# The last group's gated MLP, done for three tiles and then for the fourth

## The chip, the cores and the metric

The kernel runs on one core of a Trainium2 chip. The metric is the device time of one execution in microseconds (us), as the median of several executions; lower is better. Engines are named as the profile names them: PE is TensorE (PEld its weight loads), DVE is VectorE, ACT is ScalarE, POOL is GpSimd, SP issues the DMAs. SBUF is the on-chip memory, PSUM the memory into which PE writes.

## The reference, cut to what matters

The input x has 2 sequences of 1024 tokens with 128 channels. A stack of six blocks is applied to it, each behind a layer norm and added to x: a mixture of experts, an attention, the mixture again, a two-layer local transformer, a linear attention, and the same local transformer once more. The change is in the last block, in the second of its two layers:

```python
x = x + 0.5 * _L1_ffn_ref(_layernorm(x), ...)     # the last block: two layers of

def _layer(x, wqkv, qs, ksc, wo, lg, lb, w1, b1, w2, b2):
    ...                                           # local attention, gives o
    x = x + o @ wo
    h = shift_token(x)                            # channels 64.. from the token before
    mu = h.mean(-1, keepdims=True)
    var = h.var(-1, keepdims=True)
    h = (h - mu) / jnp.sqrt(var + 1e-05) * lg + lb
    h = h @ w1 + b1                               # 128 -> 682
    a, g = jnp.split(h, 2, axis=-1)               # 341 products, 341 gates
    h = a * jax.nn.gelu(g, approximate=False)
    x = x + h @ w2 + b2                           # 341 -> 128
    return x
```

So the gated MLP of a token needs the attention's result for this token and the one before it. All data are float32.

## The kernel before, in words

The 2048 tokens lie in 16 tiles of 128 tokens (one token a partition), eight a sequence. Four tiles make a group (`G = 4`); the function `local` works through the groups in the order of layer `l`, sequence `b` and half `c`, so (1, 1, 1) is the last group of a block. `x` holds the sum over blocks, `y` the running value inside the local transformer; both stay in SBUF.

The order of the work is written out by hand. `at(key, fn, *args)` puts a call into a plan, the plan is sorted by key, and the calls are made in that order; each engine executes its instructions in the order in which they were issued, waiting on semaphores for the others. A group starts at a key `n0`; tile k of it has the keys `n0 + k + d` with d from the list `per_tile`, and the group's MLP has `n0 + 7 + d` with d from `per_group`.

Per tile, the attention ends with these steps: `upright` (PE transposes the weights of attention, into two PSUM banks), `stood` (ACT copies them to SBUF), `weigh` (PE, 16 small matmuls `av_f`), `out_kept` (ACT copies the result to oT, L1171), `out_projected` (PE, `pj_f`, L1177), `added` (DVE adds it to the tile's y, L1183).

Per group, the MLP has: `lower_half` (POOL copies channels 0 to 63 of y to `h`, L1191), `shifted` (PE moves channels 64 to 127 down by one token: L1202, L1204, L1205), `upper_half` (ACT copies that to `h`, L1209), five pieces of the norm (`norm_h`: statistics on DVE L153 and L155, negative mean on POOL L158, root as Ln and Exp on ACT L162 and L163, offset on POOL L166, scaling on ACT L141, one instruction a tile), `inner_turned` (PE transposes, L1224), `inner_kept` (ACT, scale and shift of the norm, to `hn`, L1229), `gates` (PE: three chunks of gates of 128, 128 and 85 rows, L1239, and the third chunk of products, L1240), `gelus` (ACT, L1247; then the table of functions is set back for Ln and Exp), `third` (DVE multiplies the third products with their gates, L1253), `others` (PE: the first two chunks of products, `aa_f`, L1264), `first_two` (DVE, L1253), `outer` (PE: 12 matmuls to 128 channels, `po_f`, L1277), `second_bias` (POOL adds b2 to y, L1218) and `outer_added` (DVE adds `po_f` to y, L1288). In the last layer `onto_x` adds half of y to x (DVE, L1322) and, where `store` is set, which holds for the last block alone, issues the group's write to DRAM (SP, L1324).

In the last group all steps of the MLP have keys behind the `added` of its fourth tile. The late steps of group (1, 1, 0), from `others` on, fall in the same stretch.

PSUM has three rings: `bank2` gives pairs of banks from two buffers, `bankT` single banks from two, `bankO(name, 0 or 1)` two single ones. A new tile waits for the readers of the one that it replaces. SBUF tiles of one tag are reused in the same way; `t1` (1024 columns, two buffers) holds a tile's queries and keys until they are transposed.

Of the kernel before, what the change touches and what calls it, by code (L numbers as in the profile page):

```python
# [8 lines left out]
F32 = mybir.dt.float32  # L9
# [5 lines left out]
P = 128  # L15
# [16 lines left out]
def macaron_kernel(ctx: ExitStack, tc: tile.TileContext, a: dict, out: bass.AP):  # L32
# [14 lines left out]
    def bank2(name):  # L47
        return psA.tile([P, 2, 512], F32, tag="A", name=name)
# [6 lines left out]
    def bankO(name, which=None):  # L55
        if which is None:
            turn[0] ^= 1
            which = turn[0]
        return psO.tile([P, 512], F32, tag=f"O{which}", name=name)
# [890 lines left out]
    def at(key, fn, *args):  # L950
        plan.append((key, len(plan), lambda: fn(*args)))
# [5 lines left out]
    def tiles_of(b, c):  # L957
        return b * TB + G * c
# [7 lines left out]
    def local(name, steps, normed, store):  # L966
# [304 lines left out]
        def outer(l, b, c):  # L1271
            _, hh = mids.pop((l, b, c))
            w2 = lw[l][3]
            po = ps_["o", l, b, c] = bank2(f"po_{name}{l}{b}{c}")[:, 0, :]
            for t in range(G):
                for j, (o, n) in enumerate(HCH):
                    nc.tensor.matmul(  # L1277
                        po[:, t * P : (t + 1) * P],
                        lhsT=hh[:n, j, t * P : (t + 1) * P],
                        rhs=w2[:n, j, :],  # L1280
                        start=(j == 0),
                        stop=(j == 2),
                    )

        def outer_added(l, b, c):
            i0 = tiles_of(b, c)
            yf = y[:, i0 : i0 + G, :].rearrange("p t d -> p (t d)")
            nc.vector.tensor_tensor(yf, ps_.pop(("o", l, b, c)), yf, ALU.add)  # L1288

        per_tile = [  # L1290
            (-0.310, project), (-0.310, squares), (-0.048, cosines), (-0.024, sines), (0.212, least_norm),
# [12 lines left out]
        for (l, b, c), n0 in steps.items():  # L1304
            if l == 0:
                for part, d in enumerate(normed[b, c]):
                    at(d, norm, b, c, part)
            at(n0 - (0.626 if l == 0 else 1.519), channels, l, b, c)
            at(n0 + 0.307, keys_of_group, l, b, c)
            for k in range(G):  # L1310
                for d, fn in per_tile:
                    at(n0 + k + d, fn, l, b, G * c + k)
            for d, fn, *more in per_group:
                at(n0 + 7 + d, fn, l, b, c, *more)
            if l == 1:
                at(n0 + 11.707, onto_x, b, c, store)

    def onto_x(b, c, store):
# [380 lines left out]
```

## Time and profile before

| | us |
|---|---|
| median of 3 runs | 1902.21 (1901.45 to 1903.34) |
| the profiled execution's own time | 1902.45 |
| its span | 1900.7 |
| busy PE, DVE, ACT, POOL | 1831.6, 1402.9, 1136.0, 1136.9 |
| `added` of the fourth tile of the last group ends | 1878.3 |
| last write issued | 1897.38 |

Times inside the span count from its start. The page gives busy time and its share of the span for each engine; the chain that ended last follows the work back from the last instruction, at each step to what released it. In a list in order of time a row has start, duration, engine, line, operation, result and sources, the number of instructions merged into it and, in brackets, how long the engine had been idle and what ended that. A matmul in float32 appears as two records, a transpose as one. The ends of matmuls are modelled.

### The profile page before, as it was taken

Reading aid. Unit: us, or ns where it says so; the run is one execution under the profiler, and the core shown is the slowest. Engines: PE = TensorE matmul, PEld = TensorE weight load, DVE = VectorE, ACT = ScalarE, POOL = GpSimd, SP = SyncE. Lnnn points to the kernel's source line nnn. Section 1 sums busy time; section 2 is a strip of 40 time slices with the busy share of each in tenths; the row PEclk is TensorE's granted clock in tenths of the full one; section 3 lists DMA queues with packets and bytes.
Section 4 is the critical chain, followed back from the end, with each engine's and each line's share of the span. In section 5 each row is a group of like instructions: output and inputs, shape, how many; then the busy total and the mean of one; then the engine's idle time right before and its main releaser. Section 6 shows DMA issues by size and latency. Waiting matters only on the chain.

```text
span 1900.7 us, 37595 instructions
## 1 busy us (share of the span) xinstructions
PE 1831.6 (96%) x14482; PEld 1188.3 (63%) x14482; DVE 1402.9 (74%) x2450; ACT 1136.0 (60%) x2087; POOL 1136.9 (60%) x1036
## 2 busy tenths in 40 slices
PE   8999999999999999999999989999999899999997
PEld 5564666556665666556556556677756566676775
DVE  5748667776778667776763568888887788888884
ACT  3325555565566555565654457777676467677775
POOL 4544434343534434344444479888886689788883
PEclk8998999999999999999999999999999999999999
DMA  5331101010101101012013211111100000011110
GB/s 133 107 89 23 24 12 35 9 26 12 34 12 23 23 13 34 8 27 72 1 43 112 76 34 32 24 27 24 27 18 16 7 18 18 21 26 24 26 35 26
DMA packets 52414, 64.14 MB, mean 34 GB/s; under 512 B 17890, under 2 KB 26892, under 8 KB 51980
## 3 DMA queue, kind: packets, MB, share of 16 engines
q1 hardware_dynamic: 52236, 61.74, 12.7%
q8 instruction: 115, 1.88, 0.4%
q14 instruction: 63, 0.52, 0.1%
HBM read 27.89 MB, written 1.31 MB: 15 GB/s over the span
## 4 chain that ended last, share of the span: by engine, by line
PE 69%; ACT 12%; DVE 10%; POOL 5%; issue 4%; DMA 0%; SPq 0%; DVEq 0%; ACTq 0%; POOLq 0%
PE s L650 11%; PE tp L700 10%; PE av L717 9%; PE qk_f L989 4%; ACT p L679 4%; PE gu_m L284 3%; PE gu_m L285 3%; PE tp_f L1147 2%; PE pq L598 2%; PE acc_m L268 2%; PE s_f L1100 2%; PE av_f L1161 2%; PE v_f L1067 2%; PE po_f L1277 2%; PE tq_f L1056 2%
## 5 line engine op out<-in xcount | busy, mean ns | idle before, releaser
L686 POOL TENSOR_SCALAR p<-p,den 128x1024 f32<-128x1024 f32 x256 | 292.1, 1153 | 399.0 <-DVE den L684 313.8
L679 ACT ACTIVATE p<-p,nm 128x1024 f32<-128x1024 f32 x256 | 294.7, 1151 | 357.5 <-DVE nm L666 341.2
L666 DVE CUSTOM_DVE_ANT_0 p<-s,bias 128x1024 f32<-128x1024 f32 x256 | 302.7, 1219 | 104.0 <-PE s L650 101.4
L700 PEld LDWEIGHTS tp<-ident,p 128*128 128x128 f32 x2048 | 226.6, 141 | 100.2 <-issue 38.8
L700 PE MATMUL tp<-ident,p 128*128 128x128 f32 x2048 | 276.9, 278 | 12.2 <-ACT pt L704 10.8
L650 PE MATMUL s<-qk,qk 64*128 64x512 f32 x1024 | 258.0, 617 | 3.7 <-DVE nm L666 3.7
L717 PE MATMUL av<-pt,v 128*64 128x256 f32 x2048 | 249.1, 385 | 0.0
L706 DVE COPY pt<-tp 128x512 f32<-128x512 f32 x256 | 176.2, 688 | 92.6 <-PE tp L700 92.2
L717 PEld LDWEIGHTS av<-pt,v 128*64 128x64 f32 x2048 | 135.9, 136 | 150.0 <-issue 83.7
L1035 POOL TENSOR_TENSOR t_f<-t_f,t_f 128x1024 f32<-128x1024 f32 x64 | 151.2, 2362 | 13.6 <-DVE t_f L1021 10.0
L308 POOL TENSOR_TENSOR h_m<-h_m,cb_m 128x512 f32<-128x512 f32 x64 | 88.3, 1382 | 117.3 <-DVE h_m L304 81.5
L704 ACT COPY pt<-tp 128x512 f32<-128x512 f32 x256 | 147.5, 576 | 4.3 <-PE tp L700 3.9
L650 PEld LDWEIGHTS s<-qk,qk 64*128 64x128 f32 x1024 | 89.0, 186 | 88.1 <-issue 84.6
L1139 POOL TENSOR_TENSOR s_f<-s_f,sm_f 128x1024 f32<-128x1024 f32 x64 | 121.4, 1897 | 35.5 <-DVE sm_f L1135 33.4
L1040 POOL TENSOR_TENSOR t_f<-t_f,rn_f 128x1024 f32<-128x1024 f32 x64 | 122.3, 1911 | 12.3 <-ACT ktok L1471 8.5
L989 PE MATMUL qk_f<-wqkv,hT 128*128 128x512 f32 x256 | 123.8, 606 | 3.2 <-DVE hT L983 1.9
L1125 POOL TENSOR_TENSOR s_f<-s_f,mx_f 128x1024 f32<-128x1024 f32 x64 | 123.3, 1926 | 0.4 <-DVE mx_f L1120 0.4
L300 ACT ACTIVATE h_m<-gu_m 128x512 f32<-128x512 f32 x72 | 42.8, 597 | 127.3 <-PE gu_m L285 125.1
L1002 ACT ACTIVATE t_f<-qk_f 128x1024 f32<-128x1024 f32 x64 | 65.5, 1024 | 88.7 <-PE qk_f L989 68.8
L304 DVE TENSOR_TENSOR h_m<-h_m,gu_m 128x512 f32<-128x512 f32 x72 | 49.1, 684 | 80.8 <-ACT h_m L300 80.7
L614 POOL TENSOR_TENSOR rot<-rot,rot 128x512 f32<-128x512 f32 x32 | 40.7, 1271 | 88.0 <-DVE rot L609 88.0
L1152 ACT COPY pt_f<-tp_f 128x512 f32<-128x512 f32 x128 | 68.6, 586 | 40.4 <-PE tp_f L1147 39.6
(376 smaller groups left out, 3773.2 us busy)
## 6 DMA issues: line engine op xcount, KB each, us to landing
cb_m<-cwd_m SPq DMA_DIRECT2D x128, 128.0 KB, 3.0
qk<-rot SPq DMA_DIRECT2D x256, 64.0 KB, 2.0
tab<-in_xpos_dram SPq DMA_DIRECT2D x2, 1024.0 KB, 4.8
wqkv<-in_L_ffn_wqkv_dram SPq DMA_DIRECT2D x2, 768.0 KB, 6.4
x<-in_L_attn_x_dram SPq DMA_DIRECT2D x4, 256.0 KB, 3.5
wraw<-in_qkv_wT_dram SPq DMA_DIRECT2D x2, 512.0 KB, 4.9
vb_f<-vo_f SPq DMA_DIRECT2D x8, 128.0 KB, 2.3
out_dram<-x SPq DMA_DIRECT2D x4, 256.0 KB, 2.4
```

Source lines behind the costliest of these rows:

```text
L650: nc.tensor.matmul(pss[r][:, c, :], lhsT=qT[rows[r], t * P : (t + 1) * P], rhs=kT[rows[r], c * 512 : (c + 1) * 512], start=True, stop=True,)
L666: nc.vector.tensor_tensor_reduce(out=s, in0=pss[r].rearrange("p a n -> p (a n)"), in1=bias[r][:, o : o + S], scale=-1.0, scalar=3.0e38, op ...
L679: nc.scalar.activation(s, s, AF.Exp, bias=nm[:, r : r + 1], scale=-1.0, accum_out=den[:, r : r + 1])
L686: nc.gpsimd.tensor_scalar(probs[i, r], probs[i, r], den[:, r : r + 1], 1.0, ALU.mult, ALU.mult)
L700: nc.tensor.transpose(tp[:, k * P : (k + 1) * P], s[:, kb * P : (kb + 1) * P], ident)
L704: nc.scalar.copy(dst, src)
L706: nc.vector.tensor_copy(dst, src)
L717: nc.tensor.matmul(po[r * 64 : r * 64 + 64, 0 : 2 * P], lhsT=v[:, kb, r * 64 : r * 64 + 64], rhs=pts[i // 2, r, g][:, kb - 4 * g, :], star ...
L989: nc.tensor.matmul(ps[:, s, :], lhsT=hTs[b][:, n * P : (n + 1) * P], rhs=lw[l][0][:, s * INNER : (s + 1) * INNER], start=True, stop=True,)
L1035: nc.gpsimd.tensor_tensor(t1, t1, t2, ALU.add)
L1040: nc.gpsimd.tensor_tensor(t3, t3, rn.unsqueeze(2).to_broadcast([P, 2 * HL, 64]), ALU.mult)
L1125: nc.gpsimd.tensor_tensor(s3, s3, mx.unsqueeze(2).to_broadcast([P, HL, P]), ALU.subtract)
```

## The change

The last group of the last block no longer takes its MLP's steps from `per_group`. A new function `tail` plans them in two parts: "a", the first three tiles, and "b", the fourth.

- The lower half, shift, upper half and norm of part a have keys from the third tile's `added` on; the shift stands behind the last tile's `upright` and ahead of its `weigh`, the copy of the upper half behind `stood`, and the root and scaling behind `out_kept`.
- Everything else of the group, and the late steps of group (1, 1, 0) (`second_bias`, `others`, `first_two`, `outer`, `outer_added`, `onto_x`), stand behind the fourth tile's `added` in the order of the list `order`. The outer product of group (1, 1, 0) comes behind the gates of part a, its bias behind the norm of part b.
- Part a has gates with the third products, and the first two products later (`others_of`); part b has gates and all products in one step, in one pair of banks.
- The gates' results lie in two tiles of tag `t1` instead of one of tag `hh`, of which one is still in use by group (1, 1, 0). The outer products take banks of `bankO`.
- `bias` adds b2 to y, then `sums` adds half of y to x before the MLP's result is there; `done` adds half of the outer product to x, part by part, and issues a write for each: three tiles, then one.
- The table of functions is not set back after the last GELUs.

```diff
--- before.py
+++ after.py
@@ -1271,7 +1271,8 @@
         def outer(l, b, c):
             _, hh = mids.pop((l, b, c))
             w2 = lw[l][3]
-            po = ps_["o", l, b, c] = bank2(f"po_{name}{l}{b}{c}")[:, 0, :]
+            nm = f"po_{name}{l}{b}{c}"
+            po = ps_["o", l, b, c] = bankO(nm, 0) if store and (l, b, c) == (1, 1, 0) else bank2(nm)[:, 0, :]
             for t in range(G):
                 for j, (o, n) in enumerate(HCH):
                     nc.tensor.matmul(
@@ -1286,6 +1287,140 @@
             i0 = tiles_of(b, c)
             yf = y[:, i0 : i0 + G, :].rearrange("p t d -> p (t d)")
             nc.vector.tensor_tensor(yf, ps_.pop(("o", l, b, c)), yf, ALU.add)
+
+        def tail(n0, earlier):
+
+
+            l, b, c = 1, 1, 1
+            i0 = tiles_of(b, c)
+            ys, xs = y[:, i0 : i0 + G, :], x[:, i0 : i0 + G, :]
+            parts = {"a": slice(0, 3), "b": slice(3, 4)}
+            cols = {"a": slice(0, 384), "b": slice(384, 512)}
+            got = {}
+
+            def lower(p):
+                t = parts[p]
+                if p == "a":
+                    got["h"] = work.tile([P, G, C], F32, tag="h", name=f"h_{name}_last")
+                nc.gpsimd.tensor_copy(got["h"][:, t, 0:64], ys[:, t, 0:64])
+
+            def shift(p):
+                n = parts[p].stop - parts[p].start
+                sp = got["s", p] = bankT(f"sh_{name}_last{p}").rearrange("p (k d) -> p k d", d=64)[:, 0:n, :]
+                nc.tensor.matmul(sp, lhsT=down_one, rhs=ys[:, parts[p], 64:C], start=True, stop=False)
+                if p == "a":
+                    nc.tensor.matmul(sp[:, 0, :], lhsT=last_first, rhs=late[l, b], start=False, stop=False)
+                    sp, before = sp[:, 1:3, :], ys[:, 0:2, 64:C]
+                else:
+                    before = ys[:, 2:3, 64:C]
+                nc.tensor.matmul(sp, lhsT=last_first, rhs=before, start=False, stop=True)
+
+            def upper(p):
+                h = got["h"][:, parts[p], :]
+                nc.scalar.copy(h[:, :, 64:C], got.pop(("s", p)))
+                got["n", p] = norm_pieces(h, parts[p].stop - parts[p].start, f"f{name}_last{p}", h)
+
+            def norm_of(p, k):
+                got["n", p][k]()
+
+            def bias():
+                nc.gpsimd.tensor_tensor(ys, ys, lw[l][5].unsqueeze(1).to_broadcast([P, G, C]), ALU.add)
+
+            def sums():
+
+                nc.vector.scalar_tensor_tensor(xs, ys, 0.5, xs, ALU.mult, ALU.add)
+
+            def turn(p):
+                tp = got["t", p] = bankT(f"tf_{name}_last{p}")
+                for k in range(parts[p].start, parts[p].stop):
+                    nc.tensor.transpose(tp[:, k * P : (k + 1) * P], got["h"][:, k, :], ident)
+
+            def keep(p):
+                if p == "a":
+                    got["hn"] = work.tile([P, G * P], F32, tag="hn", name=f"hn_{name}_last")
+
+                    room = [work.tile([P, 1024], F32, tag="t1", name=f"hh{k}_{name}_last", bufs=2) for k in range(2)]
+                    got["hh", "a"] = [room[0][:, 0:384], room[0][:, 512:896], room[1][:, 0:384]]
+                    got["hh", "b"] = [room[1][:, (k + 4) * P : (k + 5) * P] for k in range(3)]
+                gb = lw[l][6]
+                hn, tp = got["hn"][:, cols[p]], got.pop(("t", p))[:, cols[p]]
+                nc.scalar.activation(hn, tp, AF.Identity, bias=gb[:, 1:2], scale=gb[:, 0:1])
+
+            def product(ps, o, m, p):
+                nc.tensor.matmul(ps, lhsT=lw[l][2][:, o : o + m], rhs=got["hn"][:, cols[p]], start=True, stop=True)
+
+            def gates_of(p):
+                first = bank2(f"ag_{name}_last{p}")
+                if p == "a":
+                    second, n = bank2(f"ah_{name}_last{p}"), 384
+                    gs = [first[:, 0, 0:n], first[:, 1, 0:n], second[: HCH[2][1], 0, 0:n]]
+                    vs = [None, None, second[: HCH[2][1], 1, 0:n]]
+                else:
+                    gs = [first[:m, 0, k * P : (k + 1) * P] for k, (_, m) in enumerate(HCH)]
+                    vs = [first[:m, 1, k * P : (k + 1) * P] for k, (_, m) in enumerate(HCH)]
+                for (o, m), ps in zip(HCH, gs):
+                    product(ps, HID + o, m, p)
+                for (o, m), ps in zip(HCH, vs):
+                    if ps is not None:
+                        product(ps, o, m, p)
+                got["g", p] = gs, vs
+
+            def gelus_of(p):
+                for k, ps in enumerate(got["g", p][0]):
+                    m = HCH[k][1]
+                    nc.scalar.activation(got["hh", p][k][:m], ps, AF.Gelu, bias=lw[l][4][:m, 1, k : k + 1])
+                written.append("gelu")
+
+            def gated_of(p, ks):
+                for k in ks:
+                    m, ps = HCH[k][1], got["g", p][1][k]
+                    hh = got["hh", p][k][:m]
+                    nc.vector.scalar_tensor_tensor(hh, ps, lw[l][4][:m, 0, k : k + 1], hh, ALU.add, ALU.mult)
+
+            def others_of(p):
+                ps = bank2(f"aa_{name}_last{p}")
+                for k in range(2):
+                    got["g", p][1][k] = ps[:, k, 0:384]
+                    product(ps[:, k, 0:384], k * P, P, p)
+
+            def outer_of(p):
+                po = got["o", p] = bankO(f"po_{name}_last{p}", 1 if p == "a" else 0)
+                for t in range(parts[p].start, parts[p].stop):
+                    for k, (_, m) in enumerate(HCH):
+                        nc.tensor.matmul(
+                            po[:, t * P : (t + 1) * P],
+                            lhsT=got["hh", p][k][:m, (t - parts[p].start) * P : (t - parts[p].start + 1) * P],
+                            rhs=lw[l][3][:m, k, :],
+                            start=(k == 0),
+                            stop=(k == 2),
+                        )
+
+            def done(p):
+                xp = xs[:, parts[p], :].rearrange("p t d -> p (t d)")
+                nc.vector.scalar_tensor_tensor(xp, got.pop(("o", p))[:, cols[p]], 0.5, xp, ALU.mult, ALU.add)
+                nc.sync.dma_start(out=ov[:, i0 + parts[p].start : i0 + parts[p].stop, :], in_=xs[:, parts[p], :])
+
+            off = {fn.__name__: d for d, fn in per_tile}
+            third_in = n0 + 2 + off["added"]
+            last_in = n0 + 3 + off["added"]
+            up, st, ok = (n0 + 3 + off[k] for k in ("upright", "stood", "out_kept"))
+            at(third_in + 0.0001, lower, "a")
+            at(max(third_in, up) + 0.0002, shift, "a")
+            at(max(third_in, st) + 0.0003, upper, "a")
+            at(max(third_in, st) + 0.0004, norm_of, "a", 0)
+            at(max(third_in, st) + 0.0005, norm_of, "a", 1)
+            for k in range(2, 5):
+                at(max(third_in, st, ok) + 0.0001 * (4 + k), norm_of, "a", k)
+            bias_, others_, first_two_, outer_, outer_added_, onto_ = earlier
+            order = [
+                others_, (lower, "b"), (shift, "b"), (upper, "b"), (turn, "a"), (keep, "a"), first_two_,
+                *[(norm_of, "b", k) for k in range(5)], bias_, (gates_of, "a"), (gelus_of, "a"), (bias,),
+                (gated_of, "a", (2,)), outer_, (turn, "b"), (keep, "b"), outer_added_, onto_, (sums,),
+                (others_of, "a"), (gated_of, "a", (0, 1)), (gates_of, "b"), (gelus_of, "b"),
+                (gated_of, "b", range(3)), (outer_of, "a"), (done, "a"), (outer_of, "b"), (done, "b"),
+            ]
+            for k, (fn, *more) in enumerate(order):
+                at(last_in + 0.0001 * (1 + k), fn, *more)
 
         per_tile = [
             (-0.310, project), (-0.310, squares), (-0.048, cosines), (-0.024, sines), (0.212, least_norm),
@@ -1310,9 +1445,14 @@
             for k in range(G):
                 for d, fn in per_tile:
                     at(n0 + k + d, fn, l, b, G * c + k)
+            ends = (second_bias, others, first_two, outer, outer_added)
             for d, fn, *more in per_group:
-                at(n0 + 7 + d, fn, l, b, c, *more)
-            if l == 1:
+                if not (store and l == b == 1 and (c == 1 or fn in ends)):
+                    at(n0 + 7 + d, fn, l, b, c, *more)
+            if store and l == b == 1:
+                if c == 1:
+                    tail(n0, [(fn, 1, 1, 0) for fn in ends] + [(onto_x, 1, 0, store)])
+            elif l == 1:
                 at(n0 + 11.707, onto_x, b, c, store)
 
     def onto_x(b, c, store):
```

## The prediction

> **What bounds the kernel now.** I read the page first, then the chain that ended last, then the instructions of the last 30 us in order of time, because the change touches nothing earlier: in the order of the two built programs every engine's stream is the same until the last tile's attention.
>
> ```profile
> span 1900.7 us, 37595 instructions
> ...
> PE 1831.6 (96%) x14482; PEld 1188.3 (63%) x14482; DVE 1402.9 (74%) x2450; ACT 1136.0 (60%) x2087; POOL 1136.9 (60%) x1036
> ...
> PE 69%; ACT 12%; DVE 10%; POOL 5%; issue 4%; DMA 0%; SPq 0%; DVEq 0%; ACTq 0%; POOLq 0%
> ...
> qk<-rot SPq DMA_DIRECT2D x256, 64.0 KB, 2.0
> ...
> out_dram<-x SPq DMA_DIRECT2D x4, 256.0 KB, 2.4
> ```
>
> TensorE (PE) is busy for 96% of the span and carries 69% of the chain, so over the whole run only less TensorE work would help. The tail is another regime: one group's MLP is alone and each engine waits for the one before it. These are its rows (start, duration, engine, line, operation), the first two of the group before:
>
> ```profile
> 1869.14 1.28 ACT L1247 ACT_TABLE_LOAD   x1
> ...
> 1870.44 1.26 ACT L1247 ACTIVATE hh_f<-ag_f,bi 128x512 f32<-128x512 f32 x2
> ...
> 1873.82 1.07 ACT L1152 COPY pt_f<-tp_f 128x512 f32<-128x512 f32 x2
> ...
> 1876.18 0.58 ACT L1171 COPY oT_f<-av_f 128x512 f32<-128x512 f32 x1 [1.29 <-PE av_f L1161]
> ...
> 1876.82 1.16 PE L1177 MATMUL pj_f<-wo,oT_f 128*128 128x128 f32 x8 [0.73 <-ACT oT_f L1171]
> ...
> 1877.81 1.88 PE L1264 MATMUL aa_f<-hn_f,wi 128*128 128x512 f32 x4
> ...
> 1879.73 1.41 DVE L1253 SCALAR_TENSOR_TENSOR hh_f<-aa_f,bi,hh_f 128x512 f32<-128x512 f32 x2 [1.43 <-PE aa_f L1264]
> ...
> 1880.13 0.54 PE L1205 MATMUL sh_f<-y,last_first 128*128 128x192 f32 x2
> ...
> 1881.20 2.72 PE L1277 MATMUL po_f<-w,hh_f 128*128 128x128 f32 x22 [0.17 <-DVE hh_f L1253]
> ...
> 1883.29 1.65 ACT L141 ACTIVATE h_f<-h_f,nb_ff,rs_ff 128x128 f32<-128x128 f32 x4 [0.38 <-POOL nb_ff L166]
> ...
> 1885.36 0.78 ACT L1229 ACTIVATE hn_f<-tf_f,gb 128x512 f32<-128x512 f32 x1 [0.42 <-PE tf_f L1224]
> ...
> 1886.15 1.28 ACT L1247 ACT_TABLE_LOAD   x1
> ...
> 1886.19 1.99 PE L1239 MATMUL ag_f<-hn_f,wi 128*128 128x512 f32 x4 [0.87 <-ACT hn_f L1229]
> ...
> 1888.21 1.26 ACT L1247 ACTIVATE hh_f<-ag_f,bi 128x512 f32<-128x512 f32 x2 [0.78 <-PE ag_f L1239]
> ...
> 1891.65 1.41 DVE L1253 SCALAR_TENSOR_TENSOR hh_f<-aa_f,bi,hh_f 128x512 f32<-128x512 f32 x2 [0.26 <-PE aa_f L1264]
> ...
> 1892.54 3.29 PE L1277 MATMUL po_f<-w,hh_f 128*128 128x128 f32 x24 [0.93 <-DVE hh_f L1253]
> ...
> 1895.94 0.69 DVE L1288 TENSOR_TENSOR y<-po_f,y 128x512 f32<-128x512 f32 x1 [2.88 <-PE po_f L1277]
> ...
> 1896.66 0.69 DVE L1322 SCALAR_TENSOR_TENSOR x<-y,x 128x512 f32<-128x512 f32 x1
> ...
> 1897.38 0.38 SPq L1324 DMA_DIRECT2D out_dram<-x  x1
> ```
>
> The reader is to see a single chain: oT copied at 1876.18, output projection, y, shift, statistics, normalisation (1883.29), hn (1885.36 to 1886.14), gates, GELUs, gating, outer product, two DVE passes, and the write issued at 1897.38. The span closes 3.3 us behind it. From 1886.14 TensorE waits three times, while its work for the group before (1881.20, 2.7 us) was done earlier, in the shade of the normalisation.
>
> One more row prices a product of 384 columns, which exists in the linear attention:
>
> ```profile
> 1385.67 1.56 PE L1374 MATMUL lp<-aw,xnTl 128*128 128x384 f32 x4
> ```
>
> Four records, of which a follower starts every 0.32 (512 columns: 0.43 each, from 1886.72, 1887.15, 1887.58 of the weight loads).
>
> **The change, part by part.** The sum goes against the profiled execution: span 1900.7 us, its own time 1902.45, 0.24 above the median of 1902.21, so a difference in span is taken off the median.
>
> Step 1: Shift of three tiles ahead of the last `weigh`. It needs y of the third tile (DVE 1873.49) and the bank that the first copy of 1873.82 frees (1874.36). The six records take 1.14 us in the row of 512 columns in all (1879.53 to 1880.67), 0.2 of it the result's way out; 384 columns take 0.21 less, so TensorE is free at 1875.14. In the old order `weigh` got going at 1874.94, when the second copy ended. Price 0.20, on the path. Queued behind it are `weigh`, oT and y of the fourth tile: oT ends 1876.96, its projection starts 1877.02. On ScalarE the copy of the shift (1875.4, 0.32) stands ahead of oT (1876.39), and ends in time. It could be nothing (both wait for the same copies) or 0.7 (the whole block); I take 0.20.
>
> Step 2: Norm of three tiles beside the last attention. Copy until 1875.7, statistics 3 x 0.31 until 1876.7, roots behind oT 1876.98 to 1877.5, POOL 0.35, three normalisations 1.27: done 1879.2. Their transposes come on TensorE behind projection (0.99), aa of the earlier group (4 x 0.43) and the fourth tile's shift (0.3), at 1880.03. Slack 0.8, so the norm costs nothing; what covers it is TensorE's own queue, and every us past those 0.8 would be paid. Transposes 0.35 and 0.2 on the way, then hn for 384 columns. A ScalarE row of 1024 elements takes 1024 ns and one of 512 597, 0.83 ns an element, so 0.78 becomes 0.67: 1880.64 to 1881.31. Gates of the three start at 1881.36 instead of 1886.19: 4.8 us earlier, the gain of the change.
>
> Step 3: What TensorE then has to do. In the new order: gates of three tiles 8 x 0.32 + 0.1 = 2.66; the earlier group's outer product, moved here, 24 records of 0.115 (22 in 2.72 less the way out) = 2.76; the fourth tile's transpose 0.12; the other two products 4 x 0.32 = 1.28; the fourth tile's six products 12 x 0.115 = 1.38, by the output projection's pace (8 records in 0.99, same shape). Sum 8.20, without a gap: until 1889.56. The bounds for the short product are 0.11 (transposes) and 0.43 (a 512-column one); the projection is the same shape, so its row is taken.
>
> Step 4: ScalarE. Statistics of the fourth tile come on DVE behind the earlier group's gating (until 1881.34); roots until 1882.25, POOL until 1882.6, normalised 1883.15, then the table load, 1.28, which began at 1886.15 and now begins at 1883.15. GELUs of three 1884.42 to 1885.96 (0.57, then 0.47 each, as 0.68 and 0.58 for 512). Third product gated on DVE until 1886.5, hn of the fourth tile 1887.1 to 1887.6, before TensorE asks for it at 1888.2. Slack 0.5 on both.
>
> Step 5: DVE, the next thing late. The earlier group's outer product now ends at 1886.98 instead of 1883.9. Behind it stand its addition, its sum onto x, and the new sum of y into x ahead, 0.72 each from the rows at 1895.94 and 1896.66; then the two gatings, 0.59 each (0.705 for 512 columns at 1.04 ns an element): until 1890.32. The sum ahead takes the place of one pass at the end, but here it is not free: TensorE is ready at 1889.56 and waits 0.8. POOL's two bias passes (1.27 each) run from 1882.7 to 1885.3, over 1.6 before DVE wants them; its bias of the earlier group, once at 1872.14, goes past nothing that is late.
>
> Step 6: The end. The first of the outer product's k = 1 matmuls starts at 1890.37; eleven more of 0.23 and 0.3: done 1893.2. GELUs of the fourth tile 1889.76 to 1890.64 and gatings until 1891.6 lie beside it, 0.6 ahead. One DVE pass of 128 columns, 0.28, instead of two of 0.69. Write issued at 1893.53: 3.85 earlier. SP gets one DMA more, its 0.38 lying before the last pass ends; the earlier group's write moves from 1885.40 to about 1888.4 and SP then has nothing until 1893. The last write is 64 KB instead of 256: the rows give 2.0 (rotary pieces) and 2.4. I take 2.05, 0.35 less; the bounds are nothing less, and 0.5 more if it queues behind the 192 KB issued at 1893.15.
>
> Sum: the gates start 4.83 earlier, with the 0.20 of step 1 already in it; from the gates to the write, 11.19 (1886.19 to 1897.38) becomes 12.17, so 0.98 is given back; the write gives 0.35. That is 4.2 us less, 1898.0.
>
> [...] The trace: the load at 1869.14 starts within 0.02 of the copy before it, takes 1.28, and the GELU follows at 1870.44. [...]
>
> **The rivals.**
> The table load holds the GELUs longer. Before, the product was what the GELU waited for (0.78 of idle at 1888.21), so an extra behind the load could have hidden there; now the products are ready at 1882.9 and nothing covers it. For it: the new place on the path. Against: 1870.44. A second length of the load, 1.28, would use up the 0.45 of DVE's slack and add 0.83: 1898.8. [...]
>
> Slower: weight loads set the pace of short products. Each product of the MLP loads weights, 0.19 us, and the next load starts 0.43 after the last. If that period were the load's and not the 512 columns', the fourth tile's shift and all products of both parts, 28 records, would take 0.43 each: 12.0 instead of 5.5, so TensorE ends 6.5 later, 0.8 of it inside DVE's lateness, and the write of 1893.5 comes at 1899.2: 1903.7. It decides from (5.5 + 0.8 + 4.2) / 28 = 0.38 a record. Against: four loads of the 384-column row in 0.94, and the projection's eight in 0.97.
>
> The gain is hidden. If y's fourth tile and not hn were what ends last, the three tiles would win nothing and the split only add. For it: both parts share TensorE's queue behind the same oT, and the last three matmuls need the fourth tile. Against: step 4 and 6 put the fourth tile 0.5 and 0.6 ahead everywhere. Each us it is later beyond that is paid; the whole gain needs 4.8. A delay of 1.5 gives 1899.0.
>
> **How the numbers follow.** The forecast has 0.84, by itself 1896.8 to 1899.2: 0.4 for the paces of steps 1 to 3, 0.3 for the short DVE and ScalarE forms, 0.3 for the write, and the spread of 1901.45 to 1903.34 on both kernels. Table load 0.06, hidden gain 0.05, weight loads 0.05. To leave out no more than 2 in 10 the range goes to 1896.3 and 1900.8. A change under 0.2%, 3.8 us, is about what a measurement of this kernel can't tell from none; the forecast lies 0.4 beyond that, so 0.70 of its 0.84 count as faster and 0.14 as no change. The table load and a hidden gain (0.11) are no change; of the weight loads 0.01 is too, and 0.04 is left for slower, for a pace above 0.43.
>
> **What would show it.** In the new profile: shift of three tiles at 1874.4 and oT not over 0.3 later; gates of three at 1881.4; no gap in TensorE from there until 1889.6; GELU directly behind the table load near 1884.4; DVE's five passes back to back from 1887.0; the last write issued near 1893.5 and the span 4.2 shorter. It is wrong if gates start after 1882, if the products' followers start over 0.35 apart, or if the last three matmuls wait for the gating of the fourth tile.

## The result, and the profile after

The changed kernel takes 1897.67 us (median of 9 executions, 1896.18 to 1900.26) against 1902.85 (9 executions, 1901.45 to 1903.93) of the kernel before: a ratio of 0.9974, 95% interval 0.9965 to 0.9983. That is 5.2 us faster, where 4.2 was forecast; 1897.67 lies 0.3 under the 1898.0 of the forecast and in its range. The profiled execution took 1896.90, its span is 1895.2.

The page of the changed kernel, in the same lines as before: TensorE's sum went down by 3.7 us (1.1 of them in the last stretch told below, 19.27 to 18.19), the chain's shares are as they were, and of the four writes of 256 KB three are left (the fourth is now one of 192 KB and one of 64).

```profile
span 1895.2 us, 37645 instructions
...
PE 1827.9 (96%) x14498; PEld 1187.8 (63%) x14498; DVE 1402.1 (74%) x2454; ACT 1136.0 (60%) x2093; POOL 1137.6 (60%) x1039
...
PE 69%; ACT 12%; DVE 10%; POOL 5%; issue 4%; DMA 0%; SPq 0%; DVEq 0%; ACTq 0%; POOLq 0%
...
out_dram<-x SPq DMA_DIRECT2D x3, 256.0 KB, 2.4
```

The span is 5.5 us shorter, but not all of it belongs to the change. I measure the changed part from a mark that both kernels reach by the same instructions in the same order: the table load of line 127, behind which the last tile's attention ends. This load starts at 1872.52 in the trace before and at 1871.35 in the trace after. From it to the end of the span are 28.19 us before and 23.85 after: **4.34 us is what the change moved in these two profiles**. The other 1.17 us lie ahead of the mark, in code that is the same; the last section comes back to them. "The last stretch" is this time below, and "mark + 8.43" is a time counted from the mark. Two profiles of the changed kernel give 23.85 and 23.84 for it. The mark in the trace of the kernel before:

```profile
1872.52 1.28 ACT L127 ACT_TABLE_LOAD   x1
```

The last stretch of the changed kernel in order of time (start, duration, engine, line, operation, result and sources, count, and in brackets the idle time with what ended it):

```profile
1871.35 1.28 ACT L127 ACT_TABLE_LOAD   x1
...
1873.28 0.59 PE L1310 MATMUL sh_f_lasta<-y,down_one 128*128 128x192 f32 x2 [0.91 <-ACT pt_f L1152]
...
1873.88 0.44 PE L1316 MATMUL sh_f_lasta<-y,last_first 128*128 128x128 f32 x2
...
1874.24 0.34 PE L1161 MATMUL av_f<-pt_f,vb_f1116n 128*64 128x64 f32 x4
...
1875.50 0.58 ACT L1171 COPY oT_f<-av_f 128x512 f32<-128x512 f32 x1 [0.83 <-PE av_f L1161]
...
1876.89 1.26 ACT L141 ACTIVATE h_f_last<-h_f_last,nb_ff_lasta,rs_ff_lasta 128x128 f32<-128x128 f32 x3 [0.37 <-POOL nb_ff_lasta L166]
...
1879.24 0.50 PE L1336 MATMUL tf_f_lasta<-ident,h_f_last 128*128 128x128 f32 x3
...
1879.78 0.67 ACT L1347 ACTIVATE hn_f_last<-tf_f_lasta,gb 128x384 f32<-128x384 f32 x1
...
1880.50 1.56 PE L1350 MATMUL ag_f_lasta<-hn_f_last,wi 128*128 128x384 f32 x4 [0.76 <-ACT hn_f_last L1347]
...
1882.32 1.28 ACT L1371 ACT_TABLE_LOAD   x1
...
1883.19 2.84 PE L1278 MATMUL po_f<-w,hh_f 128*128 128x128 f32 x24
1883.62 1.05 ACT L1371 ACTIVATE hh_f_last<-ag_f_lasta,bi 128x384 f32<-128x384 f32 x2
...
1886.14 0.69 DVE L1289 TENSOR_TENSOR y<-po_f,y 128x512 f32<-128x512 f32 x1 [0.36 <-PE tf_f_lastb L1336]
...
1886.86 0.69 DVE L1462 SCALAR_TENSOR_TENSOR x<-y,x 128x512 f32<-128x512 f32 x1
...
1887.27 1.49 PE L1350 MATMUL ag_f_lastb<-hn_f_last,wi 128*128 128x128 f32 x12
1887.47 0.68 DVE L1331 SCALAR_TENSOR_TENSOR x<-y,x 128x512 f32<-128x512 f32 x1
...
1888.07 1.13 DVE L1378 SCALAR_TENSOR_TENSOR hh_f_last<-aa_f_lasta,bi,hh_f_last 128x384 f32<-128x384 f32 x2
...
1888.74 2.58 PE L1390 MATMUL po_f_lasta<-w,hh_f_last 128*128 128x128 f32 x18
...
1889.26 1.86 PEld L1390 LDWEIGHTS po_f_lasta<-w,hh_f_last 128*128 128x128 f32 x16 [0.23 <-DVE hh_f_last L1378]
1889.70 0.86 DVE L1378 SCALAR_TENSOR_TENSOR hh_f_last<-ag_f_lastb,bi,hh_f_last 128x128 f32<-128x128 f32 x3 [0.49 <-ACT hh_f_last L1371]
...
1891.15 0.83 PE L1390 MATMUL po_f_lastb<-w,hh_f_last 128*128 128x128 f32 x6
...
1892.02 0.29 DVE L1400 SCALAR_TENSOR_TENSOR x<-po_f_lastb,x 128x128 f32<-128x128 f32 x1
```

What is to be seen, from the top. The six records of the first shift (1873.28, four of them shown) hold TensorE until the weighing starts at 1874.24, and oT follows at 1875.50. The normalisation of three tiles (1876.89) ends at 1878.15, while TensorE gets to their transposes at 1879.24 only, so it was hidden. hn starts at 1879.78, mark + 8.43 (before: mark + 12.84), the gates at 1880.50, mark + 9.15 (before: 13.67). The table load at 1882.32 is followed by the GELU within 0.02. TensorE then has no gap until the fourth tile's products end, at 1888.76. VectorE is what is late: its passes run in a row from 1886.14, and the outer product starts at 1888.74 with two records and then waits for the second gating, until 1889.26. The fourth tile's gating ends at 1890.56, before TensorE wants it at 1891.15.

### The profile page after: what moved, and what is told of

Its sections match the earlier page's. It is cut to its first block, busy times and chain, and to the rows that moved or that the text cites. A ratio compares the mean times of both kernels' runs of the same rounds, so it can differ in the third digit from the quotient of the medians.

```text
span 1895.2 us, 37645 instructions
## 1 busy us (share of the span) xinstructions
PE 1827.9 (96%) x14498; PEld 1187.8 (63%) x14498; DVE 1402.1 (74%) x2454; ACT 1136.0 (60%) x2093; POOL 1137.6 (60%) x1039
## 3 DMA queue, kind: packets, MB, share of 16 engines
q8 instruction: 115, 1.88, 0.4%
## 4 chain that ended last, share of the span: by engine, by line
PE 69%; ACT 12%; DVE 10%; POOL 5%; issue 4%; DMA 0%; SPq 0%; DVEq 0%; ACTq 0%; POOLq 0%
PE s L650 10%; PE tp L700 10%; PE av L717 9%; PE qk_f L989 4%; ACT p L679 4%; PE gu_m L284 3%; PE gu_m L285 3%; PE tp_f L1147 2%; PE acc_m L268 2%; PE s_f L1100 2%; PE av_f L1161 2%; PE pq L598 2%; PE v_f L1067 2%; PE po_f L1278 2%; PE tq_f L1056 2%
```

## The experiments

All of these kernels compute the whole output. Each is compared by its last stretch, since the time of one execution also carries what happens ahead of the mark.

**The change once more.** The same kernel as a yardstick for the others.

> The changed kernel as it is, timed beside the others: 4.3 us under the kernel before by its last stretch; the other 0.9 of the first comparison came from the stretch ahead of it, in which both kernels have the same instructions, and should not return.

Last stretch 23.84 us, with hn, gates, GELUs and the last pass of VectorE at the same distances from the mark as before within 0.01. The time is 1897.12 (5 executions, 1895.64 to 1897.76) against 1902.94 (9 executions, 1902.04 to 1904.08): ratio 0.9968, interval 0.9956 to 0.9981. So the yardstick holds for the last stretch. The other half of the expectation failed: the part beyond 4.3 did return, the medians lie 5.8 us apart.

**The sum ahead alone, in the old order.** On the kernel before, the last group's bias is added earlier, half of y goes into x ahead of the MLP's result, and one pass and one write of four tiles stand at the end:

```diff
+        def sums(l, b, c):
...
+            nc.vector.scalar_tensor_tensor(xs, ys, 0.5, xs, ALU.mult, ALU.add)
+
+        def done(l, b, c):
...
+            nc.vector.scalar_tensor_tensor(xs, ps_.pop(("o", l, b, c)), 0.5, xs, ALU.mult, ALU.add)
+            nc.sync.dma_start(out=ov[:, i0 : i0 + G, :], in_=x[:, i0 : i0 + G, :])
...
+                    if fn is outer_added:
+                        continue
+                    if fn is second_bias:
+                        at(n0 + 7 + 2.0, fn, l, b, c)
+                        at(n0 + 7 + 2.58, sums, l, b, c)
+                        continue
...
+                at(n0 + 11.707, done, l, b, c)
```

> The kernel before with one part of the change alone: b2 is added and half of y summed into x before the last group's outer product, so that one DVE pass stands behind it instead of two; no split in three tiles and one, one write of four. Measured on the last stretch: from the start of the table load that stands ahead of the last attention's copies (1872.52 before, 1871.35 with the change) to the end of the span, 28.2 us before and 23.8 with the change. Theory (the gain is the early start of three tiles): one pass of 0.7 is saved, last stretch 27.5. Rival (the shorter end makes the gain): under 26.

> The kernel before with the sum ahead alone, once more. In the first run of it the granted clock was 0.5 for 3.4 us from 1886.2 on, in which the last group's gates took 0.85 us a record instead of 0.43; its last stretch was 29.1 with that and 27.5 without those 1.6. Theory: at full clock 27.5, one pass of 0.7 under the kernel before. Rival (the moved sum itself slows the gates): 29.1 again, at full clock.

Last stretch 29.11 and 29.06 us: longer than the 28.19 of the kernel before, though the end is one pass shorter. The rows of the first one say why. Its end does what it should (one pass, then the write), but the gates, which need 1.99 us in the kernel before, take 3.58:

```profile
1885.97 3.58 PE L1239 MATMUL ag_f<-hn_f,wi 128*128 128x512 f32 x4 [0.87 <-ACT hn_f L1229]
...
1897.35 0.69 DVE L1298 SCALAR_TENSOR_TENSOR x<-po_f,x 128x512 f32<-128x512 f32 x1 [2.81 <-PE po_f L1277]
1898.07 0.38 SPq L1299 DMA_DIRECT2D out_dram<-x  x1
```

Four records of 0.43 became records of 0.85: TensorE's granted clock was 0.50 from 1886.2 to 1889.6. In the repeat such a window of 3.4 us lies elsewhere, from mark + 4.31. The first expectation failed on something that was in none of the theories, and it opened the question of the next experiment.

**The kernel before, twice more.** Is the half clock an accident of these two, or of the old last stretch?

> The kernel before as it is, for its granted clock in the last stretch. Theory one: the half clock of the first run with the sum ahead comes to this tail by chance of its phase, as both have the same waits of TensorE there: last stretch 28.2 at full clock or about 29.8 with 3.4 us at 0.5. Theory two: it belongs to the moved sum, and this kernel has 28.2 each time.

> The same kernel a second time, since one execution shows one phase: 28.2 or about 29.8 as in the run ahead.

Last stretch 29.77 and 29.86 us, against 28.19 in the first profile of the same kernel, and each has one window of 3.4 us at half clock, from mark + 4.14 and mark + 4.32. Busy time by stretches in the first of the two (stretch, length, busy time of PE, PEld, DVE, ACT and POOL with counts, granted clock, DMA share, GB/s), and the rows of TensorE in the slow one:

```profile
1873.40:1876.80 3.40, 1.80 (x35) 1.28 (x33) 0.26 (x2) 2.10 (x4) 0.19 (x1) 1.00 0.00 0
1876.80:1880.20 3.40, 3.21 (x10) 2.54 (x11) 0.29 (x1) 0.14 (x1) 0.40 (x1) 0.51 0.02 5
1880.20:1883.60 3.40, 3.23 (x16) 2.13 (x15) 2.08 (x6) 0.37 (x1) 0.00 (x0) 0.99 0.00 0
```

```profile
1876.99 2.08 PE L1177 MATMUL pj_f<-wo,oT_f 128*128 128x128 f32 x8 [0.73 <-ACT oT_f L1171]
...
1878.86 2.58 PE L1264 MATMUL aa_f<-hn_f,wi 128*128 128x512 f32 x4
```

The projection takes 2.08 instead of 1.16 and the four products 2.58 instead of 1.88. So **the profile that the forecast was made from is the exception**: of five profiles with the old last stretch (three of the kernel before, two with the sum ahead alone) it is the only one without such a window. The window costs 1.58 and 1.67 us (29.77 and 29.86 less 28.19). Against the second of these, the sum ahead alone has 29.06 with the window at the same place: 0.80 less, about one pass of VectorE with its issue (0.72). So the shorter end accounts for some 0.8 in the old order, and the smaller last write, which this kernel does not have, for 0.5 (below). The rest of the 4.34 is put down to the early start of the three tiles, whose gates come 4.51 earlier in the trace, and to the order of what follows; no run has the one without the other.

**The place of the sum.** The forecast had the sum ahead as a pass that isn't free where it stands. Behind the gating, in its place:

```diff
-                (gated_of, "a", (2,)), outer_, (turn, "b"), (keep, "b"), outer_added_, onto_, (sums,),
-                (others_of, "a"), (gated_of, "a", (0, 1)), (gates_of, "b"), (gelus_of, "b"),
+                (gated_of, "a", (2,)), outer_, (turn, "b"), (keep, "b"), outer_added_, onto_,
+                (others_of, "a"), (gated_of, "a", (0, 1)), (sums,), (gates_of, "b"), (gelus_of, "b"),
```

> The changed kernel with the sum of y into x placed behind the gating of the three tiles' first two products instead of ahead of it. Theory (the sum ahead stands on DVE's path, TensorE is ready 0.8 earlier): the matmuls of the three tiles' outer product start 0.6 to 0.7 earlier and the last stretch is 23.2 against 23.8. Rival (the sum is hidden as it stands, TensorE sets the pace): 23.8.

And no sum ahead at all, with two passes for each part at the end:

```diff
-                nc.vector.scalar_tensor_tensor(xp, got.pop(("o", p))[:, cols[p]], 0.5, xp, ALU.mult, ALU.add)
+                yp = ys[:, parts[p], :].rearrange("p t d -> p (t d)")
+                nc.vector.tensor_tensor(yp, got.pop(("o", p))[:, cols[p]], yp, ALU.add)
+                nc.vector.scalar_tensor_tensor(xp, yp, 0.5, xp, ALU.mult, ALU.add)
```

> The changed kernel without the sum ahead: the end has two DVE passes for each part again (outer product onto y, y onto x). Theory: DVE's path before the outer product is shorter by 0.72, and behind it 0.8 longer (the three tiles' second pass of 0.59 delays the fourth tile's two): last stretch 23.9, as good as the change. Rival (the sum ahead is a plain gain of a pass): 24.5.

Last stretch 23.30 with the sum behind the gating and 23.96 without it, beside 23.85. VectorE's and TensorE's rows with the sum behind, in order of time:

```profile
1885.32 0.69 DVE L1462 SCALAR_TENSOR_TENSOR x<-y,x 128x512 f32<-128x512 f32 x1
...
1885.93 1.14 DVE L1378 SCALAR_TENSOR_TENSOR hh_f_last<-aa_f_lasta,bi,hh_f_last 128x384 f32<-128x384 f32 x2
...
1886.98 0.68 DVE L1331 SCALAR_TENSOR_TENSOR x<-y,x 128x512 f32<-128x512 f32 x1
1887.05 2.17 PE L1390 MATMUL po_f_lasta<-w,hh_f_last 128*128 128x128 f32 x18
...
1888.16 0.86 DVE L1378 SCALAR_TENSOR_TENSOR hh_f_last<-ag_f_lastb,bi,hh_f_last 128x128 f32<-128x128 f32 x3 [0.49 <-ACT hh_f_last L1371]
```

The gating stands directly behind the second pass, TensorE's eighteen records have no hole (2.17 us for 2.58), and the sum itself runs while VectorE would be idle. So the sum as the change places it costs 0.55 of the 0.66 that it saves at the end: it is worth 0.11 there (23.96 to 23.85), and 0.66 one place later (23.96 to 23.30).

**The table load.** A second load of another set of functions directly ahead of the first:

```diff
             def gelus_of(p):
+                if p == "a":
+                    nc.scalar.preload_act_table_set("silu_and_others")
```

> The changed kernel with one more load of the table of functions, 1.28 us, ahead of the three tiles' GELUs. Theory: the GELUs end 1.3 later, of which DVE's wait for the earlier group's outer product covers 0.4: last stretch 24.7 against 23.8. Rivals: the load is hidden altogether, 23.8; the GELUs are on the path without slack, 25.1.

Last stretch 24.69, 0.84 more. ScalarE's and VectorE's rows around the two loads, in order of time:

```profile
1883.10 1.28 ACT L1370 ACT_TABLE_LOAD   x1
...
1884.39 1.28 ACT L1373 ACT_TABLE_LOAD   x1
1885.68 1.05 ACT L1373 ACTIVATE hh_f_last<-ag_f_lasta,bi 128x384 f32<-128x384 f32 x2
...
1887.23 0.61 DVE L1380 SCALAR_TENSOR_TENSOR hh_f_last<-ah_f_lasta,bi,hh_f_last 85x384 f32<-85x384 f32 x1 [5.58 <-ACT hh_f_last L1373]
1887.77 0.68 DVE L1289 TENSOR_TENSOR y<-po_f,y 128x512 f32<-128x512 f32 x1
```

Two loads in a row start 1.29 apart and the GELU follows 1.29 after the second. So in these rows a load costs its 1.28 and no more than 0.01 behind it, and of one load more 0.44 disappears in slack: 0.36 of idle VectorE ahead of 1886.14 in the changed kernel, and 0.08 because a pass that follows another directly starts that much before its end. The slack is now used up: VectorE's gating of the third product starts at 1887.23, and its next pass waits for that (1887.77) and no longer for TensorE.

**The earlier group's outer product ahead of the gates.** The same TensorE work with one step moved:

```diff
-                *[(norm_of, "b", k) for k in range(5)], bias_, (gates_of, "a"), (gelus_of, "a"), (bias,),
-                (gated_of, "a", (2,)), outer_, (turn, "b"), (keep, "b"), outer_added_, onto_, (sums,),
+                *[(norm_of, "b", k) for k in range(5)], bias_, outer_, (gates_of, "a"), (gelus_of, "a"), (bias,),
+                (gated_of, "a", (2,)), (turn, "b"), (keep, "b"), outer_added_, onto_, (sums,),
```

> The changed kernel with the earlier group's outer product on TensorE ahead of the three tiles' gates instead of behind them: the same work in the same queue. Theory: TensorE's sum is unchanged, but the GELUs then wait for the gates and DVE's gating of the third products and the fourth tile's hn come late: last stretch 24.9 against 23.8. Rival (only the sum in TensorE's queue counts): 23.8.

Last stretch 24.71, 0.86 more. The gates start at mark + 11.73 instead of 9.15, so the GELU waits 0.96 for them behind a load that had ended, VectorE comes later, and TensorE waits 0.80 for it. The rows of this kernel, in order of time:

```profile
1881.13 1.28 ACT L1371 ACT_TABLE_LOAD   x1
...
1881.88 1.46 PE L1350 MATMUL ag_f_lasta<-hn_f_last,wi 128*128 128x384 f32 x4
...
1883.37 1.05 ACT L1371 ACTIVATE hh_f_last<-ag_f_lasta,bi 128x384 f32<-128x384 f32 x2 [0.96 <-PE ag_f_lasta L1350]
...
1888.39 2.58 PE L1390 MATMUL po_f_lasta<-w,hh_f_last 128*128 128x128 f32 x18 [0.80 <-DVE hh_f_last L1378]
```

So it isn't enough that TensorE's work is early; the outer product is worth its place because it runs under the table load and the GELUs.

**One write of four tiles.**

```diff
-                nc.sync.dma_start(out=ov[:, i0 + parts[p].start : i0 + parts[p].stop, :], in_=xs[:, parts[p], :])
+                if p == "b":
+                    nc.sync.dma_start(out=ov[:, i0 : i0 + G, :], in_=xs)
```

> The changed kernel with one write of four tiles at the end instead of one of three and one of one. Theory: the last write is issued at the same place and takes 0.35 to 0.45 longer to its end (256 KB for 64): last stretch 24.2 to 24.3 against 23.8. Rival: the size of the last write does not count, 23.8.

Last stretch 24.33, 0.48 more, with the end of VectorE's last pass at the same mark + 20.97. Behind it come 3.37 us, as in the kernel before (3.36), instead of 2.88. All of the difference is the last write: 64 KB against 256.

**The shift behind the weighing.** Step 1 had the shift on the path of the last tile. Behind its `weigh`:

```diff
-            at(max(third_in, up) + 0.0002, shift, "a")
+            at(n0 + 3 + off["weigh"] + 0.0002, shift, "a")
```

(with the upper half and the statistics behind oT).

> The changed kernel with the shift of three tiles on TensorE behind the last weighing instead of ahead of it, its copy and statistics behind oT. Theory: oT comes 0.5 earlier, as in the kernel before (3.66 behind the table load instead of 4.15), which is the price of the shift in its place; the norm of three tiles then ends about 0.7 later than TensorE is ready for the transposes: last stretch 24.1 against 23.8. Rival (the norm has slack enough): 23.4.

oT is back at mark + 3.66, where it was in the kernel before, so the shift's place alone made it 0.49 later. But the last stretch is 23.93, 0.08 more, where 0.3 was expected: the statistics come later, the normalisation ends at mark + 8.09 instead of 6.80, past TensorE's turn, and hn starts at 8.52 instead of 8.43. In both places that were tried the shift is paid.

**A version that beats both.** With the sum behind the gating, TensorE's remaining waits are filled with the earlier group's work: its first product ahead of the shift, its second ahead of the projection, and the outer product's first tile in the wait for hn.

```diff
+            at(max(third_in, up) + 0.00015, other, 0)
+            at(n0 + 3 + off["out_projected"] - 0.001, other, 1)
+            at(n0 + 3 + off["out_projected"] + 0.001, first_two_[0], *first_two_[1:])
             order = [
-                others_, (lower, "b"), (shift, "b"), (upper, "b"), (turn, "a"), (keep, "a"), first_two_,
+                (lower, "b"), (shift, "b"), (upper, "b"), (turn, "a"), (keep, "a"), (outer_tiles, 0, 1),
...
-                (gated_of, "a", (2,)), outer_, (turn, "b"), (keep, "b"), outer_added_, onto_, (sums,),
-                (others_of, "a"), (gated_of, "a", (0, 1)), (gates_of, "b"), (gelus_of, "b"),
+                (gated_of, "a", (2,)), (outer_tiles, 1, G), (turn, "b"), (keep, "b"), outer_added_, onto_,
+                (others_of, "a"), (gated_of, "a", (0, 1)), (sums,), (gates_of, "b"), (gelus_of, "b"),
```

> The changed kernel with three more moves: the sum of y into x behind the gating; the earlier group's two products each in one of TensorE's waits of the last attention (ahead of the three tiles' shift, and between the last weighing and the output projection) with their gating behind; and the first tile of the earlier group's outer product in TensorE's wait for hn. Theory (from hn on TensorE's queue is the path, 8.2 us of it, and before hn it is the queue behind oT): 0.6 from the sum, 0.6 because hn comes earlier, 0.7 for the three matmuls in the wait: last stretch 21.9 against 23.8, time 7 us under the kernel before. Rival (the queue is not the path, the fourth tile's norm and the table load are): 23 or more.

Last stretch 22.05, 1.80 less than the change. The time is 1895.01 us (5 executions, 1894.09 to 1896.16) against the same 1902.94: ratio 0.9958, interval 0.9944 to 0.9972; the change beside it had 1897.12. The rows of this kernel that are in new places, then the gates and the last pass:

```profile
1873.27 1.02 PE L1421 MATMUL aa_f<-hn_f,wi 128*128 128x512 f32 x2
...
1876.39 1.12 PE L1421 MATMUL aa_f<-hn_f,wi 128*128 128x512 f32 x2
...
1880.04 0.83 PE L1429 MATMUL po_f<-w,hh_f 128*128 128x128 f32 x6
...
1880.97 1.56 PE L1350 MATMUL ag_f_lasta<-hn_f_last,wi 128*128 128x384 f32 x4
...
1891.28 0.29 DVE L1400 SCALAR_TENSOR_TENSOR x<-po_f_lastb,x 128x128 f32<-128x128 f32 x1
```

The two products (1873.27, 1876.39) and six of the outer product's records (1880.04) now lie where TensorE waited for ScalarE. Gates start at mark + 8.56, 0.59 earlier; from there to the end of VectorE's last pass (1891.57, mark + 19.16) are 10.60 us, against 11.26 with only the sum moved, which is the six records (6 x 0.115 = 0.69).

## Why the prediction was right, and where it was off

Direction, range and nearly the whole sum held: 4.2 forecast, 4.34 in the two profiles. In the terms of the forecast's sum: the gates come 4.51 earlier (4.83 forecast), from there to VectorE's last pass 0.65 is given back (0.98), and the end behind it gains 0.48 (0.35). By the steps, all times from the mark:

| step | forecast | measured |
|---|---|---|
| 1: oT later by | 0.20 | 0.49 |
| 2: gates of three start | 8.84 | 9.15 |
| 3: TensorE from there, without a gap | 8.20 | 8.26, with 0.16 at the end in which the last record (0.27 at a pace of 0.11) runs out |
| 4: slack of the third gating | 0.5 | 0.36 |
| 5: VectorE's five passes | 3.34 | 3.06 |
| 5: TensorE's second matmul of the outer product | 17.85 | 17.91 |
| 6: last pass of VectorE ends | 20.98 | 20.97 |
| 6: gain behind it, from the smaller write | 0.35 | 0.48 |

The forecast's times are those of its text less 1872.52 (1881.36 gives 8.84); its last pass ends 0.03 ahead of the write at 1893.53, as in the kernel before.

Step 1 failed in size. It took the 384-column shift from the 512-column row, less 0.21, and set part of it beside the wait for the second copy: TensorE held for 0.78, from mark + 1.84. The trace: the records hold TensorE 0.96 us, from 1873.28 (mark + 1.93) to 1874.24, and the weighing could not start before. The 0.49 is past the 0.3 that the forecast gave as a sign of being wrong, and the 0.29 that it cost more has gone through TensorE's queue to the gates (0.31 late).

Step 5 failed in the other direction. I took 0.72 for every pass, as the two last passes of the kernel before start 0.72 apart. There the second reads what the first has just written, and the one such pair here is 0.72 apart as well (1886.14, 1886.86). The next two start 0.61 and 0.60 behind the one ahead, and the two gatings take 1.13 instead of 1.18. Steps 1 and 5 are off by +0.3 and -0.3 and cancel: the second matmul is at 17.91 for 17.85. That the sum came out so close is in part luck.

Steps 2, 3, 4 and 6 are as told, but for the 0.3 that step 1 hands on and the slack of step 4, 0.36 for 0.5. The pace of the short products, which the slower rival hung on, is 0.12: twelve records in 1.49 us (1887.27), twelve loads in 1.59. At 0.43 each they would take 5.2.

The rival of the table load falls by the rows of the second load and by 1882.32 and 1883.62 here: 1.28 and 0.02. No load in the last stretch has more behind it, not even the second of the two in a row, whose GELU waits for nothing else and starts 0.01 behind its end (1885.67, 1885.68). The rival of the hidden gain falls by 1890.56 against 1891.15: the fourth tile is 0.6 ahead. That the last three matmuls need it is true, and costs nothing.

What the forecast missed is the difference between profile and median. The step that failed is "a difference in span is taken off the median": it treats one profiled execution as what every execution does. The medians fell by 5.2 and 5.8 us (1902.85 to 1897.67, 1902.94 to 1897.12), the last stretch by 4.34. Four of the five profiles of the old stretch have a half-clock window of about 1.6 us in it, none of the nine with the changed one has; 4/5 of 1.6 is 1.3, and 4.34 + 1.3 is 5.6, between the two. That the windows are there in the profiles is shown. That they came as often in the timed executions is only argued: their clock is known as a mean over the span. It was 0.9900 on average in the nine executions of the kernel before beside the repeat and 0.9912 in the ten of the change and of the last version, and one window of 3.4 us at half clock in 1900 makes 0.0009, so the means fit one window less, at a rounding of 0.001; but the first profiles of the two kernels have ten and eight times 3.41 us at 0.50 ahead of the mark, and the means can't say where the missing one was. There is a rival: the mark itself lies at 1872.09 us on average in the five profiles of the old order and at 1871.07 in the nine of the new one, and this 1.0 us ahead of the mark would fill the same gap. No run takes the two apart, so the cause of the part beyond 4.34 stays open.

## What to carry to other kernels

Where a last group is alone and every engine waits for the one before it, cut it by what is ready first, and put the previous group's matmuls where an engine other than TensorE is the one that everybody waits for; price each moved step by the records that it holds TensorE with, not by what it leaves out of a longer one. A pass that is taken off the end of a chain is gained only if its new place is idle: here the same pass was worth 0.11 or 0.66 us, one place apart. Before a sum is made against one profiled execution, look at the granted clock of the stretch in several of them, because a stretch with waits may run at full clock in one and not in the next: here 28.19 us at a granted clock of 1.00, and 29.77 and 29.86 with 3.4 us at 0.50.

## What the runs showed of the hardware that was not expected

TensorE's granted clock dropped to 0.50 for single windows of 3.4 us in a kernel whose TensorE is busy for 96% of the time. In the last stretch, counted from the mark, and with TensorE's busy time in the 3.4 us ahead of the drop:

| profile | half clock from | busy in the 3.4 us before | last stretch |
|---|---|---|---|
| before | none | | 28.19 |
| before, again | 4.14 | 1.77 | 29.77 |
| before, once more | 4.32 | 1.61 | 29.86 |
| sum ahead alone, again | 4.31 | 1.61 | 29.06 |
| sum ahead alone | 13.91 | 2.37 | 29.11 |
| change and the others on it (nine profiles) | none | | 22.05 to 24.71 |

Drops behind TensorE's last record, as at 1899.65 in the first profile of the kernel before, are left out of the table. The place is the wait of the last tile's attention for its copies, or, in one profile, the wait for the normalisation. Of the 3.4 us ahead of each drop TensorE was busy for 1.61 to 2.37. The change fills part of the first of these waits with the shift, as the stretches of the changed kernel from mark + 0.7 on show (columns as above):

```profile
1872.05:1875.45 3.40, 2.44 (x41) 1.94 (x39) 0.94 (x7) 1.97 (x4) 0.34 (x1) 1.00 0.00 0
1875.45:1878.85 3.40, 2.71 (x12) 1.76 (x13) 0.51 (x4) 2.25 (x6) 0.62 (x3) 1.00 0.02 5
```

With a window of 3.4 us moved over the last stretch in steps of 0.3, TensorE is busy for at least 1.60 us of it in the first profile of the kernel before, for at least 2.12 in the changed kernel and for 2.49 in the version with the waits filled. That first profile has its 1.60 at mark + 0.9, the same wait as the others, and no drop. Why this execution had none is not shown.

This weakens what the change can claim. Whether the fuller wait keeps the clock up, or all nine profiles of the new order had no drop by chance, stays open. Nor does the busy time alone tell them apart: in the first profile of the kernel before, 3.41 us with 1.61 of TensorE's work (from 1124.83) are followed by no drop, while the drop at mark + 13.91 came behind 2.37, more than the 2.12 behind which the changed kernel stays at 1.00.

Stretches at 0.50 appear well ahead of the mark, too, in code that both kernels share: in the first profile of the kernel before from 8.67 (17.07 us), 148.62 (6.83), 162.27 (3.41) and 1510.53 (6.83), in that of the changed kernel from 11.33 (13.65), 141.03, 151.27, 1127.49 and 1496.13 (3.41 each). They alone don't account for the spread of the mark, 1869.8 to 1872.7 in different executions: at a mean granted clock of 0.992 over the span the mark came at 1869.81 (the sum behind the gating) and at 1872.12 (the second table load), at 0.991 at 1869.82 (no sum ahead) and at 1872.52 (the kernel before). What else moves the mark, and with it the 1.17 us between the two first profiles, stays open. A single execution's time could not have told these versions apart; the last stretch did.
